# Layer statistics and normalisation of the later token pairs: VectorE's batch-norm instructions, or ScalarE passes with an accumulator

## The chip, the core and the metric

The kernel runs on one core of one Trainium2 chip. The time is device time in microseconds for one execution of the program. A core has TensorE (matrix products, PE in the profile; PEld is its loading of weights), VectorE (DVE), ScalarE (ACT), GpSimd (POOL) and SyncE (SP), each with its own queue of instructions, which it works off in order; semaphores make one engine wait for another. TensorE writes PSUM banks, which VectorE and ScalarE read and write.

## The reference, cut to what matters

```
def _layernorm(x):                       # over the 512 features of a token
    mu = jnp.mean(x, axis=-1, keepdims=True)
    var = jnp.mean(jnp.square(x - mu), axis=-1, keepdims=True)
    return (x - mu) / jnp.sqrt(var + EPS)
...
shift, scale, gate_msa = jnp.split(silu(t) @ ada_w + ada_b, 3, axis=1)
norm = where(m, _layernorm(x) * (1.0 + scale) + shift, 0.0)
ssm_out = where(m, ssm(norm) + flipped bwd(norm), 0.0)
x = x + gate_msa * ssm_out
shift_mlp, scale_mlp, gate_mlp = jnp.split(silu(t) @ ffada_w + ffada_b, 3, axis=1)
ff_norm = _layernorm(x) * (1.0 + scale_mlp) + shift_mlp
h = gelu(ff_norm @ ff_w1 + ff_b1)        # 512 -> 1024, tanh form
return x + gate_mlp * (h @ ff_w2 + ff_b2)  # 1024 -> 512
```

x is 32 batches of 128 tokens with 512 features, in float32. This case is about the second `_layernorm`, the one ahead of the feed-forward products.

## The kernel before, in words

The first half (the masked tokens through the two small networks) is done for the chosen tokens alone, and its rows are written to DRAM. The second half, the feed-forward block over all 4096 tokens, fills the time from about 83 us to the end. It goes in 4 pairs (`p`): a pair is two sides of 4 batches, so 2 x 4 tiles of 128 tokens x 512 features. Each of the two products of a pair is computed by seven half-sized block products P1 to P7 in place of eight, with sums of blocks formed by VectorE, GpSimd and ScalarE.

*First product* (`FirstProduct`): seven streams, in the order `STREAMS = (1, 2, 5, 6, 3, 7, 4)`. Each stream `j` has two PSUM banks, `e` and `a`. A *window* `w` interleaves the stream `STREAMS[w]` (new) with the one before (old): step n = 0 to 6 is new P5, new P1, old P3, old P7, new P2, new P6, old P4. After each step the work that belongs to it is issued: a copy of `e` by ScalarE (L1137), an addition by VectorE into `e` (L1167 behind P1, L1148 behind P6), into `h` (L1153 behind P7, L1158 behind P4), copies or gelus by ScalarE behind P2 and P3 (L1181, L1085), late sums by GpSimd (L1174, L1203, L1207). A bank may be written by the next product only when these have read it.

*Second product* (`SecondProduct`): `ORDER` lists its 14 steps, P1U P5U P1V P5V P2U and so on. P5V reads block sums `s1[1]`, which `first_block(1, 2, 4)` and `first_block(1, 0, 2)` (L1257, VectorE) form from gelus of the first product. The first steps of the second product are interleaved with P3, P7 and P4 of the last stream, stream 4.

*Where the next pair's tokens are normalised.* All orders are written out by hand: an engine runs its instructions in the order in which the program issues them. `put(w, n, f)` files work behind step n of window w. During pair p < 3 the tiles of pair p + 1 are gathered (`take_first_half`, GpSimd DMAs), then `Statistics.one(i)` takes mean and variance of a tile with VectorE's `bn_stats` and `bn_aggr` (L922, L923), and `root` adds EPS (L927, VectorE) and takes the power -0.5 for four tiles (L928, GpSimd). `blocks(side, i)` normalises a tile (L934, VectorE) and turns it in blocks of 32 x 32 (L1481, `nc.vector.transpose`). For side 0 the four calls of `blocks` stand between the last steps of stream 4, for p > 0 thus:

```
now.late_gelu("21")
blocks(0, 0); blocks(0, 1)
now.do(4, "P3"); second.seed(1); now.do(4, "P7")
second.first_block(1, 2, 4)
blocks(0, 2)
second.step(1, late=True); now.do(4, "P4")
blocks(0, 3)
second.load_gate(1); second.first_block(1, 0, 2)
second.seed_and_second_block(0)
```

For p = 0 `blocks(0, 0)` stands there alone ahead of P3, `blocks(0, 1)` behind P7, `blocks(0, 2)` behind P4 and `blocks(0, 3)` behind `first_block(1, 0, 2)`. Side 1 is normalised in the second product's steps 2 and 3. DMAs (`to_feature_rows`, L961, from SP's and ScalarE's queues) then bring the turned blocks to rows of features, ScalarE applies scale and shift (L944), and VectorE forms the block sums of the next first product (L991). The first pair's tokens are normalised apart from this, by other functions that the change leaves alone.

Of the kernel before, what the change touches and what calls it, by code (L numbers as in the profile page):

```python
# [9 lines left out]
F32 = mybir.dt.float32  # L10
# [3 lines left out]
AF = mybir.ActivationFunctionType  # L14
ALU = mybir.AluOpType
AX = mybir.AxisListType

EPS = 1e-6
# [4 lines left out]
def kernel(  # L23
# [49 lines left out]
    nc = tc.nc  # L73
    B, S, D = x.shape
    P = 128
    assert S == P
    G = 4
# [13 lines left out]
    stp = ctx.enter_context(tc.tile_pool(name="stp", bufs=4))  # L91
# [86 lines left out]
    def group_of_tiles(name):  # L178
        return xnp.tile([P, G, D], F32, tag="xn", name=f"xn_{name}")
# [35 lines left out]
    def project(i, h, w, name, between=None, bank=(ps_o, "o"), seeded=None):  # L215

        pool, tag = bank
        po = seeded or pool.tile([P, 512], F32, tag=tag, name=f"po_{name}_{i}")
        for f in range(HC):
            if between and f in between:  # L220
                between[f]()
            nc.tensor.matmul(  # L222
                po,
                h[f][:, ts(i, P)],
                w[:, f, :],
                start=(f == 0 and seeded is None),
                stop=(f == HC - 1),
                skip_group_check=seeded is not None,
            )
        return po  # L230
# [6 lines left out]
    def gated(po, bias, gate, name):  # L237

        t = tp.tile([P, D], F32, tag="t", name=f"t_{name}")
        nc.vector.tensor_tensor(t, po, bias, ALU.add)  # L240
        nc.vector.tensor_tensor(t, t, gate, ALU.mult)
        return t
# [144 lines left out]
    class Weights:  # L387


        def __init__(self, w, rows, cols, t):  # L390
            b11, b12 = w[:, :rows, :cols], w[:, :rows, cols:]
            b21, b22 = w[:, rows:, :cols], w[:, rows:, cols:]
            t2, t3, t4 = (t[:, j] for j in range(3))
            self.sums = [(t3, b22, b12), (b12, b12, b11), (t2, b22, b12), (t4, b21, t2)]
            self.of = {
                "P1": b11, "P2": b21, "P3": b22, "P4": t4, "P5": b12, "P6": t2, "P7": t3
            }
# [321 lines left out]
    def in_blocks(t):  # L719
        return t.rearrange("p g (h f) -> p (g h) f", f=2 * P)  # L720
# [59 lines left out]
    for f in range(KC):  # L780
        hidden_of_tile(f, 1)
        for done in (f - 1, f) if f % 2 else ():
            t = ssm.tile([P, NH], F32, tag="h", name=f"h_s0_{done}", bufs=HC)
# [28 lines left out]
    t = in_blocks(group_of_tiles("tw_3"))  # L812
# [27 lines left out]
    def in_turned_blocks(t):  # L840
        return t.rearrange("p i d -> p (i d)").rearrange("p (k i c) -> p k i c", i=G, c=P)

    def normalised(row, t):
        src = row[:, :D]
        if len(t.shape) == 3:
            src = src.rearrange("p (k c) -> p k c", k=KC)
        nc.vector.tensor_scalar(
            t, src, row[:, D : D + 1], row[:, D + 1 : D + 2], ALU.subtract, ALU.mult
        )
        return t  # L850
# [3 lines left out]
    def normalised_of_side_0(which):  # L854
        for i in which:
            t = normalised(raw[i // 2][:, i % 2], xn[:, :, i])
            nc.vector.transpose(t, t)
# [51 lines left out]
    class Statistics:  # L909


        def __init__(self, src, name):
            self.src, self.name = src, name
            self.mv = stp.tile([P, G, 2], F32, tag="mv4", name=f"mv_{name}", bufs=2)
            self.rstd = stp.tile([P, G], F32, tag="rstd4", name=f"rstd_{name}", bufs=2)

        def tile_at(self, i):
            return self.src[i // 2][:, i % 2]

        def one(self, i):  # L920
            st = stp.tile([P, 6], F32, tag="st", name=f"st_{self.name}_{i}")
            nc.vector.bn_stats(st, self.tile_at(i))  # L922
            nc.vector.bn_aggr(self.mv[:, i, :], st)  # L923

        def root(self):
            ve = stp.tile([P, G], F32, tag="ve4", name=f"ve_{self.name}", bufs=2)
            nc.vector.tensor_scalar(ve, self.mv[:, :, 1], EPS, None, ALU.add)  # L927
            nc.gpsimd.tensor_tensor(self.rstd, ve, half[:, :G], ALU.pow)  # L928

        def normalised(self, i, t):  # L930
            src = self.tile_at(i)
            if len(t.shape) == 3:
                src = src.rearrange("p (k c) -> p k c", k=KC)
            nc.vector.tensor_scalar(  # L934
                t, src, self.mv[:, i, 0:1], self.rstd[:, i : i + 1], ALU.subtract, ALU.mult
            )
            return t

# [15 lines left out]
    def turned(xn, xT, queues, which=range(4)):  # L954

        R = 32
        src = xn.rearrange("p k i (q c) -> p q k i c", c=R)
        dst = xT.rearrange("p k (i b c) -> p b k i c", b=P // R, c=R)
        for b in which:
            for q in range(P // R):  # L960
                queues[(b + q // 2) % len(queues)].dma_start(dst[ts(q, R), b], src[ts(b, R), q])  # L961
# [7 lines left out]
    def new_xT(p, side):  # L969
        return xtp.tile([P, KC, G * S], F32, tag=f"xT{side}", name=f"xT_{p}_{side}")  # L970
# [390 lines left out]
    def normalised_of_side_1():  # L1361
        t = sp.tile([P, G, D], F32, tag="s12", name="xn_0_1")
        for i in range(G):
            xn_b.append(normalised(raw[2 + i // 2][:, i % 2], t[:, i]))
# [42 lines left out]
    gp = straight.enter_context(tc.tile_pool(name="gp", bufs=1))  # L1407
# [26 lines left out]
    for p in range(NP):  # L1434
# [4 lines left out]
        def put(w, n, f, *args):  # L1439
            fills.setdefault(w, {}).setdefault(n, []).append(lambda: f(*args))  # L1440
# [26 lines left out]
        if more_pairs:  # L1467
            x_next = x_of[p + 1]
            stats = [Statistics(x_next[side], f"{p + 1}_{side}") for side in range(2)]
            xn, xT = {}, {}  # L1470

            def blocks(side, i):

                if i == 0:
                    xn[side] = in_turned_blocks(
                        group_of_tiles(f"{p + 1}_0")
                        if side == 0
                        else sp.tile([P, G, D], F32, tag="s12", name=f"xn_{p + 1}_1")
                    )
                t = stats[side].normalised(i, xn[side][:, :, i])  # L1480
                nc.vector.transpose(t, t)  # L1481

            def to_feature_rows(side, *queues):
                xT[side] = new_xT(p + 1, side)
                turned(xn[side], xT[side], queues)

            if p:
                put(1, 6, take_first_half, p + 1, x_next, range(G))
            put(2, 6, take_first_half, p + 1, x_next, range(G, G + 2 + (p == 0)))
            if p:  # L1490
                put(3, 4, take_first_half, p + 1, x_next, range(G + 2, G + 3))
            put(5, 4, take_first_half, p + 1, x_next, range(G + 3, 2 * G))
            for i, at in enumerate(((3, 1), (3, 3), (3, 4), (4, 1))):
                put(*at, stats[0].one, i)
            put(*((4, 1) if p else (5, 4)), stats[0].root)
            for i, at in enumerate(((4, 4), (5, 1), (5, 3), (6, 4))):
                put(*at, stats[1].one, i)
            put(6, 6, stats[1].root)
        for w in range(1 + (p == 0), 7):
            now.window(STREAMS[w], STREAMS[w - 1], fills.get(w, {}))  # L1500
# [88 lines left out]
    with tc.If(more > 0):  # L1589
# [11 lines left out]
        with tc.For_i(0, more, 1):  # L1601
# [12 lines left out]
            for half_no, (mod, was, wbs, bias, bcol, func) in enumerate(  # L1614
# [19 lines left out]
                shift, scale, gate_l = (mod_l[:, m] for m in range(3))  # L1634
# [5 lines left out]
                t = gated(project(0, h_l, wb, f"l{half_no}"), bias, gate_l, f"l{half_no}")  # L1640
# [59 lines left out]
```

## Time and profile before

| what | before |
|---|---|
| median of 3 runs | 453.1 us (452.22 to 453.49) |
| span of the profiled execution | 451.7 us, 6204 instructions |
| PE, PEld busy | 444.0 us (98%), 370.2 us (82%) |
| DVE busy | 334.5 us (74%), 573 instructions |
| ACT busy | 177.9 us (39%), 389 instructions |
| POOL busy | 158.4 us (35%), 154 instructions |
| granted TensorE clock | 1.000 |

The span runs from the first to the last instruction of the one execution that was profiled; the times are of other executions, from outside, and hold what lies around the span as well, here some 1.4 us between the two. Rows of the timeline give start, duration, engine, line of the kernel, operation, tile written `<-` tiles read, shapes and count; in brackets stands the idle time of the engine before it and what ended it. Rows of groups give count, busy us, mean ns of one, then idle time before them. A matmul's row begins some 0.17 us before the one ahead of it ends, since they are pipelined. Rows of consecutive instructions overlap on ScalarE and VectorE also, by some 0.07 to 0.1 us.

### The profile page before, as it was taken

The numbers are of one execution on the slowest core, as the hardware profiler recorded it, in microseconds if no ns is written. First come the engines' busy times: TensorE is split into PE (matmuls) and PEld (weight loads), VectorE is DVE, ScalarE is ACT, GpSimd is POOL, SyncE is SP. The second block draws the span as 40 slices with busy tenths as digits, with TensorE's granted clock in tenths as the row PEclk, the third lists the DMA queues.
The fourth block names the chain that finished last, engine by engine and source line by source line (L and its number), as shares of the span: only waits on it lengthen the run. The fifth ranks groups of instructions, "written<-read, shape, count | busy, mean of one in ns | idle before, by whom it ended". The sixth has DMA issues, their size and how long they took to land.

```text
span 451.7 us, 6204 instructions
## 1 busy us (share of the span) xinstructions
PE 444.0 (98%) x2147; PEld 370.2 (82%) x2147; DVE 334.5 (74%) x573; ACT 177.9 (39%) x389; POOL 158.4 (35%) x154
## 2 busy tenths in 40 slices
PE   8999999999999999999999999999999999999995
PEld 3884675688888888888888888888888888888884
DVE  5797788877799759977895689878956885434645
ACT  3123116353651551536526415464265244642000
POOL 4211470089770000897600007977000027560000
PEclk9999999999999999999999999999999999999999
DMA  6999449857327717741396177512971534122022
GB/s 250 372 399 408 177 65 308 284 187 229 129 97 168 108 49 268 235 138 36 105 177 93 46 267 230 141 38 86 189 99 47 176 128 129 35 93 95 0 94 96
DMA packets 85440, 70.84 MB, mean 157 GB/s; under 512 B 63396, under 2 KB 64508, under 8 KB 84382
## 3 DMA queue, kind: packets, MB, share of 16 engines
q1 hardware_dynamic: 64270, 57.76, 42.3%
q0 software_dynamic: 4160, 10.54, 6.9%
q10 hardware_dynamic: 16976, 2.11, 3.9%
q8 instruction: 18, 0.29, 0.3%
q14 instruction: 16, 0.13, 0.1%
HBM read 56.71 MB, written 13.70 MB: 156 GB/s over the span
## 4 chain that ended last, share of the span: by engine, by line
PE 84%; DMA 8%; DVE 3%; issue 2%; POOL 1%; SPq 0%; POOLq 0%
PE a_o L1310 24%; PE a_m L1123 21%; PE e_o L1310 18%; PE e_m L1123 16%; DMA fw<-in_L_cond_ff_w_dram 3%; PE po_s L222 3%; DMA w<-in_L_cond_bwd_w_dram 3%; DMA x_wide<-t_s 2%; DMA x<-x_wide,slot_i 1%; DVE t L403 1%; PE last L1310 1%; PE a_m_alone L1123 1%; POOL x L819 1%; PE ptr L950 0%; PE pl_s L255 0%
## 5 line engine op out<-in xcount | busy, mean ns | idle before, releaser
L1174 POOL TENSOR_TENSOR ha<-p_m,ha 128x512 f32<-128x512 f32 x20 | 25.8, 1292 | 176.0 <-ACT ha L1181 166.1
L1310 PE MATMUL e_o<-fw,ha 128*128 128x256 f32 x256 | 57.9, 379 | 0.0
L944 ACT ACTIVATE xT<-xT,modT 128x128 f32<-128x128 f32 x112 | 44.0, 480 | 28.1 <-DMA xT<-xn 28.1
L1310 PE MATMUL a_o<-t,hb 128*128 128x256 f32 x240 | 54.1, 379 | 0.0
L1310 PEld LDWEIGHTS e_o<-fw,ha 128*128 128x128 f32 x256 | 48.6, 190 | 6.6
L1310 PEld LDWEIGHTS a_o<-t,hb 128*128 128x128 f32 x240 | 45.6, 190 | 6.2
L1085 ACT ACTIVATE hb<-hb,biasT 128x256 f32<-128x256 f32 x64 | 29.0, 500 | 28.3 <-POOL hb L1207 16.1
L1137 ACT COPY p_m<-e_m 128x512 f32<-128x512 f32 x27 | 15.8, 586 | 51.6 <-PE e_m L1123 51.6
L890 POOL DMA_INDIRECT x<-x_rows,slot_i x24 | 27.2, 1135 | 6.2 <-issue 5.4
L1174 POOL TENSOR_TENSOR hb<-p_m,hb 128x512 f32<-128x512 f32 x20 | 29.2, 1460 | 0.3
L1310 PE MATMUL a_o<-fw,ha 128*128 128x256 f32 x128 | 28.9, 379 | 0.0
L1310 PE MATMUL a_o<-t,s 128*128 128x256 f32 x128 | 28.9, 379 | 0.0
L1310 PE MATMUL e_o<-fw,s 128*128 128x256 f32 x128 | 28.9, 379 | 0.0
L222 PE MATMUL po_s<-w,h_s 128*128 128x512 f32 x64 | 28.4, 594 | 0.0
L1181 ACT COPY ha<-e_m 128x512 f32<-128x512 f32 x32 | 18.5, 579 | 24.8 <-PE e_m L1123 24.4
L1310 PEld LDWEIGHTS a_o<-fw,ha 128*128 128x128 f32 x128 | 24.3, 190 | 3.3
L1310 PEld LDWEIGHTS a_o<-t,s 128*128 128x128 f32 x128 | 24.3, 190 | 3.3
L1310 PEld LDWEIGHTS e_o<-fw,s 128*128 128x128 f32 x128 | 24.3, 190 | 3.3
L1148 DVE TENSOR_TENSOR e_m<-a_m,ha 128x512 f32<-128x512 f32 x20 | 14.0, 698 | 17.0 <-POOL ha L1174 7.6
L1085 ACT ACTIVATE ha<-e_m,biasT 128x256 f32<-128x256 f32 x48 | 20.0, 468 | 14.4 <-PE e_m L1123 14.4
L1123 PE MATMUL a_m<-xT,tw 128*128 128x256 f32 x96 | 24.7, 380 | 0.0
L1123 PE MATMUL e_m<-s,fw 128*128 128x256 f32 x92 | 23.7, 380 | 0.0
(234 smaller groups left out, 894.1 us busy)
## 6 DMA issues: line engine op xcount, KB each, us to landing
x<-in_x_dram SPq DMA_DIRECT2D x16, 512.0 KB, 5.9
tw<-t_rows SPq DMA_DIRECT2D x16, 512.0 KB, 4.3
gate<-gate_rows POOLq DMA_DIRECT2D x8, 1024.0 KB, 5.1
out_dram<-x SPq DMA_DIRECT2D x15, 512.0 KB, 4.7
tw<-t_rows SPq DMA_DIRECT2D x16, 384.0 KB, 3.9
xT<-xn SPq DMA_DIRECT2D x80, 64.0 KB, 2.7
ada_f<-in_L_cond_ffada_w_dram SPq DMA_DIRECT2D x4, 768.0 KB, 14.8
ada_a<-in_L_cond_ada_w_dram SPq DMA_DIRECT2D x4, 512.0 KB, 3.6
```

Source lines behind the costliest of these rows:

```text
L222: nc.tensor.matmul(po, h[f][:, ts(i, P)], w[:, f, :], start=(f == 0 and seeded is None), stop=(f == HC - 1), skip_group_check=seeded is no ...
L403: engine.tensor_tensor(out, x, y, ALU.subtract)
L819: nc.gpsimd.indirect_dma_start(out=raw[i // 2][:, i % 2], out_offset=None, in_=x1_wide[:slots], in_offset=bass.IndirectOffsetOnAxis(ap=slo ...
L890: nc.gpsimd.indirect_dma_start(out=xs[i // G][i % G // 2][:, i % 2], out_offset=None, in_=x1_rows, in_offset=bass.IndirectOffsetOnAxis(ap= ...
L944: nc.scalar.activation(out, src, AF.Identity, bias=shift, scale=scale)
L1085: nc.scalar.activation(dst[:, n], src[:, n], AF.Gelu_apprx_tanh, bias=biasT[:, f : f + 1])
L1123: nc.tensor.matmul(bank[:, ts(n, QT)], self.w_block(j, product)[:, ts(n, P)], self.x_block(j, product), start=(product in ("P1", "P5") and ...
L1137: nc.scalar.copy(p5, e)
L1148: nc.vector.tensor_tensor(e, a, p5, add)
L1174: nc.gpsimd.tensor_tensor(self.place(RESULT[j], c), self.p5[j], other, ALU.add)
L1181: nc.scalar.copy(self.place(RESULT[j], c), src)
L1310: nc.tensor.matmul(part, src[:, k, ts(i, P)], w[product][:, k, :], start=(last and k == 0), stop=True, skip_group_check=True,)
```

## The change

For the tiles of pairs 2 to 4, ScalarE reads a tile once with Identity and an accumulator for the sum (`one`), VectorE turns the sum into minus the mean (one column), ScalarE reads the tile again with Square, that column as bias and an accumulator for the sum of squares (`two`). Both passes write their 512-wide result to a tile that nobody reads. `root` divides, adds EPS (VectorE), takes the power and forms `shift` = -mean x rstd (GpSimd). `normalised` is a ScalarE Identity with scale and bias columns; the 32 x 32 transpose behind it stays on VectorE. For p > 0 `root` of side 0 moves from (4, 1) to (4, 4).

```diff
         def __init__(self, src, name):
             self.src, self.name = src, name
-            self.mv = stp.tile([P, G, 2], F32, tag="mv4", name=f"mv_{name}", bufs=2)
+            self.sums = stp.tile([P, G], F32, tag="sums4", name=f"sums_{name}", bufs=2)
+            self.minus = stp.tile([P, G], F32, tag="minus4", name=f"minus_{name}", bufs=2)
+            self.var = stp.tile([P, G], F32, tag="var4", name=f"var_{name}", bufs=2)
             self.rstd = stp.tile([P, G], F32, tag="rstd4", name=f"rstd_{name}", bufs=2)
+            self.shift = stp.tile([P, G], F32, tag="shift4", name=f"shift_{name}", bufs=2)
...
+        def unread(self):
+            return gp.tile([P, D], F32, tag="unread", name=f"unread_{self.name}", bufs=1)
+
         def one(self, i):
-            st = stp.tile([P, 6], F32, tag="st", name=f"st_{self.name}_{i}")
-            nc.vector.bn_stats(st, self.tile_at(i))
-            nc.vector.bn_aggr(self.mv[:, i, :], st)
+            nc.scalar.activation(
+                self.unread(), self.tile_at(i), AF.Identity, accum_out=self.sums[:, i : i + 1]
+            )
+            nc.vector.tensor_scalar(
+                self.minus[:, i : i + 1], self.sums[:, i : i + 1], -1.0 / D, None, ALU.mult
+            )
+
+        def two(self, i):
+            nc.scalar.activation(
+                self.unread(),
+                self.tile_at(i),
+                AF.Square,
+                bias=self.minus[:, i : i + 1],
+                accum_out=self.var[:, i : i + 1],
+            )

         def root(self):
             ve = stp.tile([P, G], F32, tag="ve4", name=f"ve_{self.name}", bufs=2)
-            nc.vector.tensor_scalar(ve, self.mv[:, :, 1], EPS, None, ALU.add)
+            nc.vector.tensor_scalar(ve, self.var, 1.0 / D, EPS, ALU.mult, ALU.add)
             nc.gpsimd.tensor_tensor(self.rstd, ve, half[:, :G], ALU.pow)
+            nc.gpsimd.tensor_tensor(self.shift, self.rstd, self.minus, ALU.mult)

         def normalised(self, i, t):
...
-            nc.vector.tensor_scalar(
-                t, src, self.mv[:, i, 0:1], self.rstd[:, i : i + 1], ALU.subtract, ALU.mult
+            nc.scalar.activation(
+                t, src, AF.Identity, bias=self.shift[:, i : i + 1], scale=self.rstd[:, i : i + 1]
             )
             return t
...
             for i, at in enumerate(((3, 1), (3, 3), (3, 4), (4, 1))):
                 put(*at, stats[0].one, i)
-            put(*((4, 1) if p else (5, 4)), stats[0].root)
+            for i, at in enumerate(((4, 1), (4, 3), (4, 3), (4, 4))):
+                put(*at, stats[0].two, i)
+            put(*((4, 4) if p else (5, 4)), stats[0].root)
             for i, at in enumerate(((4, 4), (5, 1), (5, 3), (6, 4))):
                 put(*at, stats[1].one, i)
+            for i, at in enumerate(((5, 4), (5, 5), (6, 4), (6, 6))):
+                put(*at, stats[1].two, i)
             put(6, 6, stats[1].root)
```

## The prediction

> **What bounds the kernel now.** I read the page first, then busy time by stretches, the waits of TensorE's weight loads (PEld) behind the opening, and the timelines of the engines through one pair of sides. The rows of the page:
>
> ```profile
> span 451.7 us, 6204 instructions
> ...
> PE 444.0 (98%) x2147; PEld 370.2 (82%) x2147; DVE 334.5 (74%) x573; ACT 177.9 (39%) x389; POOL 158.4 (35%) x154
> ...
> PE 84%; DMA 8%; DVE 3%; issue 2%; POOL 1%; SPq 0%; POOLq 0%
> ```
>
> Busy time by stretches (columns: length, then PE, PEld, DVE, ACT, POOL, granted clock, DMA share, GB/s), and the waits of PEld from 80 us on (total, times, longest):
>
> ```profile
> 178.00:267.00 89.00, 89.00 (x413) 77.78 (x411) 71.19 (x109) 41.28 (x91) 36.07 (x30) 1.00 0.54 139
> ```
>
> ```profile
> PEld a_m L1123 <- DVE hb L1153: 1.1, 4, 0.4
> ```
>
> The reader is to see that TensorE is never out of work between pairs: 89.00 of 89.00 us, and about a microsecond of real waiting in all. So work taken from VectorE can pay at most that microsecond, while each new wait of TensorE is paid in full. The question is not whether ScalarE has room on average (41 of 89 us) but whether, in its fixed order, it delays what TensorE needs next.
>
> **The change part by part.** What VectorE loses, in groups (count, busy us, mean ns), with the row of the transposes that stay and that of a one-column scalar operation:
>
> ```profile
> L1481 DVE STREAM_TRANSPOSE xn<-xn 128x512 f32<-128x512 f32 x24 | 17.1, 712 | 0.8
> L922 DVE BATCH_NORM_STATS2 st<-x 128x6 f32<-128x512 f32 x24 | 16.4, 682 | 0.0
> L934 DVE TENSOR_SCALAR xn<-x,mv,rstd 128x512 f32<-128x512 f32 x24 | 14.7, 613 | 0.0
> L927 DVE TENSOR_SCALAR ve<-mv 128x4 f32<-128x4 f32 x6 | 6.0, 1006 | 0.1
> L923 DVE BATCH_NORM_AGGREGATE mv<-st 128x2 f32<-128x6 f32 x24 | 4.4, 182 | 0.8
> L162 DVE TENSOR_SCALAR ve_s<-mv_s 128x1 f32<-128x1 f32 x4 | 0.6, 154 | 0.1
> ```
>
> It loses 16.4 + 4.4 + 14.7 = 35.5 us and gets 24 one-column products, 24 x 0.154 = 3.7 us. ScalarE gets 72 passes. Their prices come from these rows:
>
> ```profile
> L944 ACT ACTIVATE xT<-xT,modT 128x128 f32<-128x128 f32 x112 | 44.0, 480 | 28.1 <-DMA xT<-xn 28.1
> L1181 ACT COPY ha<-e_m 128x512 f32<-128x512 f32 x32 | 18.5, 579 | 24.8 <-PE e_m L1123 24.4
> L1386 ACT ACT_TABLE_LOAD x1 | 1.3, 1283 | 0.0
> L570 ACT ACTIVATE s_sb<-t_sb 32x512 f32<-32x512 f32 x1 | 0.6, 630 | 0.2 <-DMA t_sb<-in_cond_dram 0.2
> L575 ACT COPY sT<-ptr_s 128x128 f32<-128x128 f32 x1 | 0.3, 265 | 1.6 <-PE ptr_s L574 1.6
> ```
>
> The two copies give (579 - 265)/384 = 0.82 ns per element. A normalisation is the 128-wide Identity of L944 (scale and bias from columns) widened to 512: 480 + 384 x 0.82 = 795 ns, followed by the next after about 0.71. A sum pass is L570's 0.63 us; a squared pass with a bias column lies between that and 0.80, I take 0.72. How the accumulator is written out, no row shows: between nothing and the 0.27 of a small copy, I take 0.1 of ScalarE's time and 0.2 until the sum can be read, near its small rows. Together 24 x (0.73 + 0.82 + 0.71) = 54 us on ScalarE, 18 per pair.
>
> *Statistics, windows 3 to 6.* ScalarE's waits there are holes of about a microsecond between copies that TensorE needs, and each takes one pass. Replayed by hand for the second iteration (p = 1), pass by pass at these prices: the copies behind P3 and P2 come 0.1 to 0.8 us later, for which the next reader has more than a microsecond. Two places are tight. First, today's only clear stall here goes. VectorE's `ve` sits before the addition behind P7 of stream 6, and TensorE waits for that:
>
> ```profile
> 199.48 1.10 DVE L927 TENSOR_SCALAR ve<-mv 128x4 f32<-128x4 f32 x1
> ...
> 203.00 0.70 DVE L1148 TENSOR_TENSOR e_m<-a_m,ha 128x512 f32<-128x512 f32 x1 [1.00 <-POOL ha L1203]
> ```
>
> ```profile
> 201.23 1.13 PE L1123 MATMUL a_m<-xn_sy,tw 128*128 128x256 f32 x4
> ...
> 203.93 1.03 PE L1123 MATMUL e_m<-s,fw 128*128 128x256 f32 x4
> ```
>
> `ve` began at 199.48 and took 1.10 us; products follow each other every 0.86, and the one at 201.23 is followed by the next at 202.20, so 0.2 us were lost. With `root` moved behind, that is won. Second, VectorE now has `ve` and the product for side 1's first tile ahead of L1148. Both wait for ScalarE, where the fourth squared pass and side 1's first sum pass stand behind the gelu of P2: about 202.4 and 203.2. L1148 then starts at 203.3 instead of 203.00 and ends at 204.0, past 203.93 less the 0.2 just won: 0.2 to 0.4 lost. I book these two as zero for p = 1 and 2. For p = 0, whose `root` is not at that place and which had no such stall, I book 0.2.
>
> *Normalisation, start of the second product.* Here is the price. Today VectorE normalises and transposes alone, in between products' additions, while ScalarE works beside it. Its transposes now wait for ScalarE, where each normalisation stands behind a gelu; and the gelu behind it waits for VectorE's addition, which stands behind the transpose. ScalarE before, p = 1 (and the one row of p = 0):
>
> ```profile
> 220.04 0.91 ACT L1085 ACTIVATE hb<-hb,biasT 128x256 f32<-128x256 f32 x2 [2.14 <-POOL hb L1207]
> 220.86 0.82 ACT L1085 ACTIVATE ha<-e_m,biasT 128x256 f32<-128x256 f32 x2
> 221.57 0.59 ACT L1249 COPY a_o<-fb 128x512 f32<-128x512 f32 x1
> ...
> 222.84 0.91 ACT L1085 ACTIVATE hb<-hb,biasT 128x256 f32<-128x256 f32 x2 [0.17 <-DVE hb L1153]
> 225.22 0.91 ACT L1085 ACTIVATE hb<-hb,biasT 128x256 f32<-128x256 f32 x2 [1.47 <-DVE hb L1158]
> ```
>
> ```profile
> 129.98 0.91 ACT L1085 ACTIVATE hb<-hb,biasT 128x256 f32<-128x256 f32 x2 [2.98 <-POOL hb L1207]
> ```
>
> VectorE before:
>
> ```profile
> 220.33 0.71 DVE L1481 STREAM_TRANSPOSE xn<-xn 128x512 f32<-128x512 f32 x1
> ...
> 222.16 0.65 DVE L1153 TENSOR_TENSOR hb<-a_m,hb 128x512 f32<-128x512 f32 x1
> ...
> 224.53 0.65 DVE L1158 TENSOR_TENSOR hb<-a_m,hb 128x512 f32<-128x512 f32 x1
> ...
> 226.30 0.65 DVE L1257 TENSOR_TENSOR s<-hb 128x512 f32<-128x512 f32 x1
> ```
>
> TensorE before, p = 1 and then p = 0: P4 of stream 4, which overwrites the bank L1153 reads, and P5V, whose first weights are what the last L1257 writes:
>
> ```profile
> 222.92 1.07 PE L1123 MATMUL a_m<-xT,tw 128*128 128x256 f32 x4
> ...
> 227.28 3.62 PE L1310 MATMUL e_o<-fw,s 128*128 128x256 f32 x16
> ```
>
> ```profile
> 132.01 1.03 PE L1123 MATMUL a_m<-xT,tw 128*128 128x256 f32 x4
> ...
> 136.32 3.62 PE L1310 MATMUL e_o<-fw,s 128*128 128x256 f32 x16
> ```
>
> Today L1257 ends at 226.95, 0.33 us ahead of 227.28. The new order for p = 1, counted from t, the start of the late gelu (220.04 above). It occupies ScalarE 0.82.
> 1. Normalise tile 0 from t+0.82, tile 1 from t+1.53, done at t+2.33 (ScalarE). Transpose 1 from t+2.38 to 3.05 (0.64 to 0.71 us each).
> 2. L1153 to t+3.70; so P4 starts at t+3.75. ScalarE meanwhile: gelu pair to 3.06, two seeds to 4.1, so L1153's gelu pair runs from 4.02, and tile 2's normalisation from 4.84 to 5.64.
> 3. Transpose 2 to 6.35; L1158 to 7.00; its gelu pair 7.05 to 7.95, tile 3's normalisation from 7.87 to 8.67; transpose 3 from 8.70 to 9.40; L1257 to 10.05. P5V at t+10.1.
>
> With t = 220.04 P5V starts at 230.14, 2.9 us late; TensorE idles about 0.9 ahead of P4 and 2.0 ahead of P5V. t itself moves: the late gelu waits for GpSimd's chain of late sums, which starts with the copy behind P3 of stream 7, now some 0.7 later behind squared passes and seeds. The row of its last link:
>
> ```profile
> 218.75 1.26 POOL L1207 TENSOR_TENSOR hb<-hb 128x512 f32<-128x512 f32 x1
> ```
>
> Between 0 and 0.7, I take 0.35, since part of the chain waits for other things: 3.2 us each for p = 1 and 2. In p = 0 one tile is normalised at each place and the last L1257 stands behind three of them, each behind a gelu pair: tile 0 done t+1.62, transpose 2.35, L1153 3.00, gelu pair 3.3 to 4.2, tile 1 done 4.9, transpose 5.65, two additions 6.95, gelu pair to 7.9, tile 2 done 8.62, transpose 9.35, L1257 10.0, P5V at t+10.05. With t = 129.98 + 0.35 that is 140.4 against 136.32: 4.1 us.
>
> *Side 1 and after.* Its four normalisations are in steps 2 and 3, behind the four DMA issues of side 0 on ScalarE's queue; the fourth transpose comes about 0.4 us later against TensorE than now. The next product's P5 has 258.37 - 254.48 = 3.9 us in hand there, between the sum that it reads (VectorE) and its start (TensorE):
>
> ```profile
> 253.25 1.23 DVE L991 TENSOR_TENSOR s<-xT 128x1024 f32<-128x1024 f32 x1 [3.63 <-ACT xT L944]
> ```
>
> ```profile
> 258.37 1.03 PE L1123 MATMUL e_m<-s,fw 128*128 128x256 f32 x4
> ```
>
> So zero; if that cover is gone, each microsecond costs one. SP's queue issues the same DMAs. The throw-away output tile is written by ScalarE alone and waits for nobody. GpSimd gets six 128x4 products (`shift`), each between 0.1 and the 1.04 of the root:
>
> ```profile
> 200.66 1.04 POOL L928 TENSOR_TENSOR rstd<-ve,half 128x4 f32<-128x4 f32 x1
> ```
>
> Nearer the low end, as a power costs more than a product; zero beside the t above, to 0.9 per pair in the range.
>
> *The sum.* 4.1 + 3.2 + 3.2 + 0.2 = 10.7 us on a span of 451.7: 462.4. The median of the runs, 453.1, is 1.4 above that span (launch and spread); carried over, 463.8, which I round to 463.5.
>
> **The rivals.**
>
> *One-column products held up by GpSimd.* The row to look at is `ve`: 0.14 us in p = 0, where GpSimd had nothing in hand, but 1.10 above, where GpSimd was in an addition until 200.55:
>
> ```profile
> 116.44 0.14 DVE L927 TENSOR_SCALAR ve<-mv 128x4 f32<-128x4 f32 x1
> ```
>
> ```profile
> 199.28 1.27 POOL L1174 TENSOR_TENSOR hb<-p_m,hb 128x512 f32<-128x512 f32 x1
> ```
>
> If the 24 one-column products behave so, each costs up to 1.2 us. Three of them have no cover: side 1's first, ahead of L1148, puts P3 of stream 3 back by 1 us in each pair, and one at (6, 4) some 0.5. That is 3 to 4.5 us more: 467. Against it: no one-column product of this trace stood beside GpSimd's work, and the 0.154 row is without it. The Trainium skill (SBUF — State Buffer, "Who interferes with whom") says that VectorE's two-port modes and GpSimd lock each other out for a whole instruction, whoever is second waiting. `ve`'s 0.14 against 1.10 agrees; whether one column enters such a mode, no run here shows. Chance 0.15.
>
> *Tables.* Three table loads stand in the whole trace and Identity and Copy run between gelus without one; Square does not occur. If it needs another set, each squared pass or pair of them brings two loads of 1.283: some 18 x 2.57 = 46 us on ScalarE, of which, with holes of a microsecond, most of the half in windows 4 to 6 reaches TensorE: 485. The Trainium skill (ScalarE: Activation LUTs, "Table sets: the hidden batching unit") has cheap functions in every set; Square is not among the examples there, so this stays a rival. Chance 0.03.
>
> *No cost: the chain keeps its cover.* What decides is t: if GpSimd's chain gets shorter because VectorE no longer disputes with it, and the late gelu starts 2.9 us earlier (at 217.1 rather than 220.04), P5V is not late, the lost 0.2 us of p = 1 and 2 are won and the time is 452.7. For it speaks that L1207 at 218.75 is the end of a chain of GpSimd's additions, some of them beside VectorE's work; against it that this chain would have to lose more than two whole additions of 1.26 us, and that it starts later. Chance 0.06, of it 0.02 for more than 0.3% faster.
>
> **How the numbers follow.** The forecast has 0.76, the product rival 0.15, tables 0.03, cover kept 0.06. 0.3% is 1.4 us, about what a measurement of this kernel can tell from no change. The low end: t unmoved and normalisations as short as the 0.58 copies take 0.85 off each chain, so 3.0 + 2.0 + 2.0 = 7.0, or 460; the accumulator free, 459. The high end: the product rival, 467, with the late GpSimd products, 468.5. Faster 0.02, same 0.04, slower 0.94.
>
> **What would show it.** VectorE busy near 302 and ScalarE near 230 us. A wait of TensorE ahead of P4 of stream 4 near 1 us and ahead of P5V near 2, in three iterations and not in the fourth; VectorE's transposes waiting for ScalarE's normalisation; the 0.2 us stall behind `ve` gone. One-column products of a microsecond would show the first rival, ACT_TABLE_LOADs beyond three the second. It is wrong if P5V keeps its time, or if TensorE waits mostly in windows 3 to 6, where I booked next to nothing.

## The result and the profile after

| | before | changed |
|---|---|---|
| median of 4 runs each | 452.7 us (452.22 to 453.49) | 467.13 us (466.04 to 467.68) |
| ratio | 1 | 1.0309, 95% interval 1.0289 to 1.033 |
| span of the profiled execution | 451.7 us | 464.2 us |
| PE busy | 444.0 us | 446.6 us |
| DVE busy | 334.5 us | 306.3 us |
| ACT busy | 177.9 us | 226.5 us |

The change makes the kernel 3.1% slower: 14.4 us by the medians, 12.5 by the two profiled executions. VectorE has 28 us less to do and ScalarE 49 us more; neither is what the time goes by. The waits of TensorE itself from 80 us on (total, times, longest), of which the profile before has none:

```profile
PE e_o L1329 <- DVE s L1276: 5.8, 3, 2.3
PE a_m L1142 <- DVE hb L1172: 4.0, 3, 1.4
PE e_m L1142 <- DVE e_m L1167: 1.3, 3, 0.4
```

Three waits in each of three pairs: P5V for the last block sum (L1276, which was L1257), P4 of stream 4 for the addition ahead of it (L1172, was L1153), P3 of stream 3 for L1167 (was L1148). Lines behind the changed class are 19 higher than before. TensorE in the second iteration, with the idle time in front of each:

```profile
208.75 1.10 PE L1142 MATMUL e_m<-s,fw 128*128 128x256 f32 x4 [0.44 <-DVE e_m L1167]
...
229.38 1.13 PE L1142 MATMUL a_m<-xT,tw 128*128 128x256 f32 x4 [1.39 <-DVE hb L1172]
230.35 3.62 PE L1329 MATMUL a_o<-fw,ha 128*128 128x256 f32 x16
...
235.70 3.69 PE L1329 MATMUL e_o<-fw,s 128*128 128x256 f32 x16 [1.74 <-DVE s L1276]
```

Who waits for whom there is read off ScalarE and VectorE side by side. ScalarE, from the late gelu on:

```profile
225.69 0.91 ACT L1104 ACTIVATE hb<-hb,biasT 128x256 f32<-128x256 f32 x2 [1.42 <-POOL hb L1226]
226.50 1.50 ACT L953 ACTIVATE xn<-x,shift,rstd 128x512 f32<-128x512 f32 x2
...
229.66 0.91 ACT L1104 ACTIVATE hb<-hb,biasT 128x256 f32<-128x256 f32 x2
230.47 0.81 ACT L953 ACTIVATE xn<-x,shift,rstd 128x512 f32<-128x512 f32 x1
232.63 0.91 ACT L1104 ACTIVATE hb<-hb,biasT 128x256 f32<-128x256 f32 x2 [1.36 <-DVE hb L1177]
233.44 0.80 ACT L953 ACTIVATE xn<-x,shift,rstd 128x512 f32<-128x512 f32 x1
```

VectorE in the same time:

```profile
227.33 1.42 DVE L1500 STREAM_TRANSPOSE xn<-xn 128x512 f32<-128x512 f32 x2 [1.65 <-ACT xn L953]
228.67 0.65 DVE L1172 TENSOR_TENSOR hb<-a_m,hb 128x512 f32<-128x512 f32 x1
...
231.30 0.71 DVE L1500 STREAM_TRANSPOSE xn<-xn 128x512 f32<-128x512 f32 x1 [1.38 <-ACT xn L953]
231.94 0.65 DVE L1177 TENSOR_TENSOR hb<-a_m,hb 128x512 f32<-128x512 f32 x1
234.27 0.71 DVE L1500 STREAM_TRANSPOSE xn<-xn 128x512 f32<-128x512 f32 x1 [1.68 <-ACT xn L953]
234.90 0.65 DVE L1276 TENSOR_TENSOR s<-hb 128x512 f32<-128x512 f32 x1
```

The reader is to see two engines that take turns, three times each, from the late gelu to the block sum: VectorE is idle for 1.4 to 1.7 us ahead of each of its turns, ScalarE, which has copies to do in between, for 1.4 us ahead of its last. P5V starts when the last turn (L1276, ending at 235.55) is done.

From the starts of the four iterations on TensorE, the first pair costs 5.04 us more than before, the second 4.02, the third 4.03; with an opening 0.57 shorter that is the 12.5 us between the spans.

### The profile page after: what moved, and what is told of

It is laid out like the page before. It is cut to its first block, busy times and chain, and to the rows that moved or that the text cites. A ratio compares the mean times of both kernels' runs of the same rounds, so it can differ in the third digit from the quotient of the medians.

```text
span 464.2 us, 6305 instructions
## 1 busy us (share of the span) xinstructions
PE 446.6 (96%) x2147; PEld 369.9 (80%) x2147; DVE 306.3 (66%) x525; ACT 226.5 (49%) x509; POOL 158.3 (34%) x160
## 4 chain that ended last, share of the span: by engine, by line
PE 77%; ACT 11%; POOL 5%; issue 3%; DVE 3%; ACTq 0%; DVEq 0%
PE a_o L1329 19%; PE e_o L1329 16%; PE a_m L1142 13%; PE e_m L1142 11%; PE po_s L222 6%; PE ph_s L205 5%; ACT unread L935 2%; ACT hb L1104 2%; POOL hb L1226 2%; ACT xn L953 2%; PE ph_s L681 2%; ACT ha L1104 1%; ACT unread L927 1%; POOL hb L1193 1%; ACT ha L1200 1%
## 5 line engine op out<-in xcount | busy, mean ns | idle before, releaser
L1500 DVE STREAM_TRANSPOSE xn<-xn 128x512 f32<-128x512 f32 x24 | 17.0, 711 | 21.3 <-ACT xn L953 21.3
```

## The experiments

Theory A is the prediction's: the price is the alternation of the two engines ahead of P4 and P5V, with a small wait at P3. Rival B: ScalarE has too much to do, wherever the passes stand.

**Statistics alone.** The normalisation goes back to VectorE, and `shift` is not formed:

```diff
-            nc.scalar.activation(
-                t, src, AF.Identity, bias=self.shift[:, i : i + 1], scale=self.rstd[:, i : i + 1]
-            )
+            nc.vector.tensor_scalar(
+                t, src, self.minus[:, i : i + 1], self.rstd[:, i : i + 1], ALU.add, ALU.mult
+            )
```

> Statistics by ScalarE as in the change, normalisation back on VectorE. Theory A (the price is the alternation of ScalarE's normalisations with VectorE's transposes and additions at the start of the second product, 2.9 to 4.4 us a pair, with 0.4 to 0.7 us a pair at P3 of stream 3): P3's wait stays, 0.68 us three times; the start of the second product loses only what `ve`, now later, pushes back, 0.7 to 1.7 us a pair. Sum 3 to 6 us over before: 456 to 459 us. Rival B (the price goes with the time that ScalarE is taken, 48 us of passes, wherever they stand): the 48 statistics passes with their reads are 41 of 60 us, so about 10 of the 14 us: 462 to 463 us.

457.3 us against 453.17 of before, ratio 1.0089 (1.0073 to 1.0104). TensorE's waits from 80 us on (lines here are 17 higher than before the change: L1170 was L1153, L1165 was L1148):

```profile
PE a_m L1140 <- DVE hb L1170: 1.4, 2, 0.7
PE e_m L1140 <- DVE e_m L1165: 1.3, 3, 0.4
```

P5V does not wait; P3 waits as in the changed kernel, and P4 in two pairs, because VectorE comes later to its addition L1165 and to all that stands behind it, `ve` among it. Counted from the start of the second product, L1165 starts at 2.55 us (218.24 - 215.69) in the second iteration, where it was 1.48 (215.77 - 214.29) before; ahead of it VectorE stands waiting for ScalarE's sum of side 1's last tile:

```profile
218.13 0.15 DVE L929 TENSOR_SCALAR minus<-sums 128x1 f32<-128x1 f32 x1 [3.47 <-ACT unread L926]
```

Two thirds of ScalarE's new passes cost 4.1 of the 14.4 us, not 10: against B.

**Normalisation alone.** Statistics by VectorE as before, the shift column by two GpSimd products:

```diff
             nc.gpsimd.tensor_tensor(self.rstd, ve, half[:, :G], ALU.pow)
+            nc.gpsimd.tensor_scalar(self.shift, self.mv[:, :, 0], -1.0, None, ALU.mult)
+            nc.gpsimd.tensor_tensor(self.shift, self.shift, self.rstd, ALU.mult)
...
-            nc.vector.tensor_scalar(
-                t, src, self.mv[:, i, 0:1], self.rstd[:, i : i + 1], ALU.subtract, ALU.mult
-            )
+            nc.scalar.activation(
+                t, src, AF.Identity, bias=self.shift[:, i : i + 1], scale=self.rstd[:, i : i + 1]
+            )
```

> Statistics by VectorE as before, normalisation by ScalarE (the shift column formed by two small GpSimd products more). Theory A: the late gelu starts where it did before, P5V comes 10.1 us behind it, so 2.9 + 2.9 + 3.7 = 9.5 us over before, 0.3 less or more: 462 us; P3 of stream 3 does not wait, the waits ahead of P4 and P5V are 1 to 2.3 us. Rival B: 19 of 60 us of ScalarE's passes, so about 4.5 us: 457 us.

464.48 us, ratio 1.0241 (1.0225 to 1.0258): 11.3 us over before, with a third of the passes. B is out, but the forecast of 462 was 2.5 us too low, and P4 waited 0.6 to 0.9 us, not 1 or more. The chain has the length that was worked out: ScalarE's late gelu and TensorE's P5V of the second iteration are 10.01 us apart (forecast 10.1), and the gelu starts 5.75 us behind the start of the second product, as before (lines here are 3 higher than before the change).

```profile
225.78 0.91 ACT L1088 ACTIVATE hb<-hb,biasT 128x256 f32<-128x256 f32 x2 [2.13 <-POOL hb L1210]
```

```profile
235.79 3.69 PE L1313 MATMUL e_o<-fw,s 128*128 128x256 f32 x16 [1.73 <-DVE s L1260]
```

Most of the excess over 9.5 us in the profiled execution has its place in the first pair. There P5V took 5.38 us instead of 3.69 behind its wait, and the granted clock (the column with 1.00 in the first row) was 0.61 and 0.90 in these stretches:

```profile
139.89 5.38 PE L1313 MATMUL e_o<-fw,s 128*128 128x256 f32 x16 [2.33 <-DVE s L1260]
```

```profile
137.00:139.80 2.80, 0.56 (x3) 0.16 (x1) 1.34 (x3) 2.77 (x6) 0.00 (x0) 1.00 0.58 237
139.80:143.30 3.50, 3.41 (x10) 2.80 (x11) 2.81 (x3) 0.41 (x1) 0.00 (x0) 0.61 0.32 43
143.30:146.70 3.40, 3.40 (x16) 2.93 (x15) 1.78 (x3) 2.60 (x5) 0.00 (x0) 0.90 1.03 148
```

9.5 and this 1.7 are 11.2 us; the span is 11.8 longer than the one before, and the other 0.6 us stays open. Two other executions, at mean granted clocks of 0.998 and 0.997, which executions of the kernel before show as well, were 10.5 and 11.0 us over before; the lower clock does not explain what these have above 9.5.

**The wait at P3.** Side 1's first sum pass two steps later, in the changed kernel:

```diff
-            for i, at in enumerate(((4, 4), (5, 1), (5, 3), (6, 4))):
+            for i, at in enumerate(((4, 6), (5, 1), (5, 3), (6, 4))):
                 put(*at, stats[1].one, i)
```

> The changed kernel with side 1's first sum pass and its product on VectorE two steps later, at (4, 6) in place of (4, 4), behind the addition that P3 of stream 3 waits for. Theory A: that product, not the gelu or GpSimd's sums, holds the addition; the three waits of 0.44 us (0.68 with what the pipeline loses) go or shrink to 0.2, P4 and P5V keep theirs: 1 to 2 us under the changed kernel. Rival (the addition waits for GpSimd's late sum, as it did before): unchanged within 0.5 us.

464.94 us, ratio 1.0271 (1.0252 to 1.0289), 2.2 us under the changed kernel's median (and 1.1 to 2.1 by the executions at a clock of 1.000 alone). The waits for L1167 are gone, the others unchanged to the tenth:

```profile
PE e_o L1329 <- DVE s L1276: 5.8, 3, 2.3
PE a_m L1142 <- DVE hb L1172: 4.0, 3, 1.4
```

So it was VectorE's in-order wait for ScalarE's sum, not a GpSimd sum. In the changed kernel this is the place (VectorE):

```profile
207.80 0.15 DVE L930 TENSOR_SCALAR minus<-sums 128x1 f32<-128x1 f32 x1 [0.30 <-ACT unread L927]
207.91 0.70 DVE L1167 TENSOR_TENSOR e_m<-a_m,ha 128x512 f32<-128x512 f32 x1
```

**One link less.** The changed kernel in which VectorE normalises one of side 0's four tiles in each of the three pairs, the one whose transpose stands last:

```diff
+            if self.by_vector == i:
+                nc.vector.tensor_scalar(
+                    t, src, self.minus[:, i : i + 1], self.rstd[:, i : i + 1], ALU.add, ALU.mult
+                )
+                return t
...
+            stats[0].by_vector = 3 if p else 2
+            stats[1].by_vector = None
```

> The changed kernel, but the one tile of side 0 whose transpose stands last ahead of the final block sum (tile 3, in the first pair's iteration tile 2) is normalised by VectorE. Theory A, link by link: that tile no longer waits for the gelu pair ahead of it; VectorE normalises and turns it beside the gelu, so P5V comes 1.2 us earlier in each of three pairs: 3.6 us under the changed kernel, the wait ahead of P5V 0.6 to 1.2 us, the one ahead of P4 as it is. Rival B: one tile in eight of the normalisations, 0.8 us of 20 a pair, so under 0.7 us in all.

462.88 us, ratio 1.0208 (1.0195 to 1.0222): 4.2 us under the changed kernel's median, and 3.6, as expected, under the middle of its two executions at a clock of 1.000. P4 waits as it did, P5V 2.0 us in all instead of 5.8, so 1.27 less per pair where 1.2 was expected (lines here are 24 higher than before the change: L1177 was L1153, L1281 was L1257, L1172 was L1148):

```profile
PE a_m L1147 <- DVE hb L1177: 4.0, 3, 1.4
PE e_o L1334 <- DVE s L1281: 2.0, 3, 1.1
PE e_m L1147 <- DVE e_m L1172: 1.3, 3, 0.4
```

Three normalisations of 0.8 us, 2.4 us of ScalarE's time in all, were worth 3.8 us of waits, where rival B allowed 0.7: position, not load.

**All passes on ScalarE, in another order.** Normalisations (`normal`, ScalarE) apart from their transposes (`turn_blocks`, VectorE), which keep all their places; the other calls of `blocks` for side 0 become `turn_blocks` likewise:

```diff
-            def blocks(side, i):
+            def normal(side, i):
...
-                t = stats[side].normalised(i, xn[side][:, :, i])
+                stats[side].normalised(i, xn[side][:, :, i])
+
+            def turn_blocks(side, i):
+                t = xn[side][:, :, i]
                 nc.vector.transpose(t, t)
...
+        if more_pairs:
+            for i in range(2):
+                normal(0, i)
         now.late_gelu("21")
         if more_pairs:
             for i in range(1 + (p > 0)):
-                blocks(0, i)
+                turn_blocks(0, i)
         now.do(4, "P3")
         second.seed(1)
+        if more_pairs:
+            for i in range(2, G):
+                normal(0, i)
         now.do(4, "P7")
...
```

> The changed kernel with ScalarE's normalisations of side 0 issued apart from the transposes: tiles 0 and 1 ahead of the late gelu, where ScalarE sat idle 1.4 to 2.3 us, tiles 2 and 3 behind the seeds; VectorE's order is kept. Theory A: all 60 us of passes are still on ScalarE, but no transpose waits behind a gelu that waits for VectorE, so nearly all of the 3.6 to 4.4 us at P4 and P5V comes back, 0 to 0.5 a pair stays, and the three waits at P3 of stream 3 stay (0.44 us idle each): 1 to 3.5 us over before, 454 to 457 us. Rival B (ScalarE's load): no change beyond 1 us.

455.82 us, ratio 1.0066 (1.0052 to 1.0081): 11.3 of the 14.4 us are back with every pass still on ScalarE. Waits left:

```profile
PE e_m L1142 <- DVE e_m L1167: 1.3, 3, 0.4
PE e_o L1329 <- DVE s L1276: 0.4, 1, 0.4
```

With the later sum pass as well:

> The earlier normalisations and the later first sum pass together. Theory A: the effects add up; a further 1.5 to 2.2 us less than with the earlier normalisations alone, so 452.5 to 455 us: level with before, and not faster by more than the 0.5 us that its two stalls behind `ve` cost. Rival B: as the changed kernel.

454.25 us (12 runs), ratio 1.0030 (1.0017 to 1.0042). The two effects add up as far as can be told; one wait of 0.4 us ahead of the first pair's P5V and short waits of the weight loads are left, and it stays 1.1 us behind before. Lighter by 29 us (305.6 us busy), VectorE returns nothing.

**The clock.** Theory C was formed from the 0.61 above; two of four executions of the changed kernel were at a mean granted clock of 0.995 and 0.996, with spans of 465.9 and 465.7 us, the others at 1.000, with 464.2 and 465.1.

```diff
         for step in range(2, len(ORDER)):
+            if step == 3 and more_pairs:
+                busy = ps_t.tile([P, 512], F32, tag="tr", name=f"busy_{p}")
+                for _ in range(8):
+                    nc.tensor.matmul(busy[:, :P], ident, ident, start=True, stop=True)
             second.step(step)
```

> The changed kernel with eight 128x128 products on TensorE, whose result nobody reads, ahead of P5V in the three pairs, some 0.9 us of work within a gap of 1.7 to 2.5 us. Theory C: in some executions of the changed kernel and of the one with normalisation alone the granted clock falls behind the 2.33 us gap of the first pair and costs 1.2 to 1.7 us; with the gap cut to about 1.4 us this never happens: all executions at a clock of 0.998 or more, 465.5 to 467 us, the median 0.3 to 1 us under the changed kernel's. Rival D (the lower clock has nothing to do with the gap): about half the executions still at 0.994 to 0.996 and the median as the changed kernel's.

465.97 us (465.53 to 466.21), ratio 1.0287 (1.0274 to 1.0301); all five executions at 0.998 or more. The eight products took 1.95 us and not 0.9, so they filled more of the gap than was meant: P4's waits are the same as without them, P5V's is 0.56 us in the first pair and gone in the others, and P5V starts no later. That agrees with C: 1.2 us of the changed kernel's median, a little more than was expected.

Two executions of four and none of five are few, but all the runs here say the same. Mean granted clocks of 0.996 or less occur only in the three kernels whose profile has the gap of 2.33 us: in 2 of 4 executions of the changed kernel, 2 of 4 with normalisation alone, 2 of 5 with the later sum pass, and these took 0.6 to 1.8 us longer than the others of their kernel. In 67 executions of the other kernels, 23 of the kernel before among them, the lowest was 0.997. Only the profile of normalisation alone shows the drop in its place; that it stands at the same place in the changed kernel is probable and not shown.

**The stall of the kernel before.** `root` of side 0 at (5, 4) in all pairs, nothing else:

```diff
-            put(*((4, 1) if p else (5, 4)), stats[0].root)
+            put(5, 4, stats[0].root)
```

> The kernel before, with side 0's `root` at (5, 4) in every pair as it is in the first: the 0.24 us stall of TensorE behind `ve` goes in two pairs, 0.5 us under before (452.7 us), about what can be told from no change; the rival, GpSimd's chain moved by its power, 0 to 0.5 us slower.

452.14 us (12 runs) against 453.12 of before, ratio 0.9984 (0.9973 to 0.9995). This is the one version that is faster than both, by 0.05 to 0.27%, by taking away a wait of TensorE and not work from VectorE. In its profile the two iterations whose `root` was moved are 0.25 and 0.26 us shorter, which is the 0.5 that was expected; the rest of the 1.0 us between the medians is within the interval.

## Why the prediction was right, point by point

- *What bounds it.* TensorE's waits account for the difference: 11.1 us of idle time, and what the pipeline loses each time it starts again; 28 us less on VectorE gave back nothing, as the 89.00 of 89.00 said. The cover-kept rival and with it every gain is out.
- *Prices.* The passes took what was worked out from the narrower rows: 0.62 for a sum (0.63), 0.72 for squares (0.72), 0.80 for a normalisation (0.795); the accumulator is an instruction of its own of 0.19 (taken as 0.1 of ScalarE's time and 0.2 until the sum can be read). VectorE came to 306.3 us and ScalarE to 226.5, where 302 and 230 were forecast. A group row of ScalarE, and `shift` on GpSimd, where 0.1 to 1.04 was left open (minimum, median, maximum in ns):

```profile
L935 ACT ACTIVATION_READ_ACCUMULATOR unread<-x,minus 128x1 f32 x24 | 4.5, 188 | 0.0
```

```profile
L947 POOL TENSOR_TENSOR shift<-rstd,minus x6: 198/199/268, 121.5 to 321.9; 128x4 f32<-128x4 f32 x6
```

- *The chain.* P5V started 10.01 us behind the late gelu in the second iteration and 140.72 - 130.82 = 9.90 in the first; forecast 10.1 and 10.05. Experiments two and four confirm single links.
- *First term mis-sized: when the late gelu starts.* It was put 0.35 us later than before, between 0 and 0.7; measured from the start of the second product it is 225.69 - 219.19 = 6.50 against 5.75, and 0.75 later in the first pair too: just past the upper bound. GpSimd's late sums pass on the delay of the copy that starts them, 0.79 us at their start (218.78 - 219.19 against 213.09 - 214.29), almost whole; the part that "waits for other things" did not exist. 0.4 us a pair.
- *Second: P3 of stream 3.* The two effects there were booked as zero, 0.2 in the first pair. The wait is 0.44 us idle and 0.24 more that the pipeline loses in starting again, 0.68 in all (starts of TensorE's rows), against 0.24 won. The addition ended some 0.15 later than in the replay by hand, and the loss of restarting was left out. 0.45 us a pair. The gain was real: experiment eight shows it by itself.
- *The sum* was 10.7 us on the span and 13.1 came, 12.5 with the opening. The medians are 14.4 apart, since the changed kernel's profiled execution, 466.04 us for a span of 464.2, is the fastest of its four, and two of the four had the lower clock, which the prediction left out. The 1.4 us that it carried over from span to median was too little as well: an execution here takes 1.7 to 1.9 us longer than its span.
- *The range.* That 467.1 lies in it is in part luck. The forecast with t at its upper bound is about 1 us longer, near 465; the upper end came from the product rival, whose 467 is nearly the measured time, and from late GpSimd products, and neither occurred: these products took some 0.15 and 0.2 us each.
- *Rivals.* One-column products do not wait for GpSimd: all 24 took 149 to 156 ns, the one at 203.01 in the middle of a GpSimd addition (202.50 to 203.79). `ve`, with four columns, took 0.16 us in the first pair and 1.23 beside an addition, with which it ended (225.68 and 225.66). The rule cited from the Trainium skill agrees with that, and the runs answer what was open: one column is not held up. Square brought no table load; there are three, as before.

```profile
L930 DVE TENSOR_SCALAR minus<-sums x24: 149/153/156, 101.9 to 316.6; 128x1 f32<-128x1 f32 x24
```

## What to carry to other kernels

Before work is moved to an emptier engine, write the two queues side by side at the place where it lands: if the moved step stands between two steps of the other engine and itself behind a step that waits for that engine, the engines take turns, and each turn is paid, however idle both are. Splitting the moved step from its consumer and issuing it earlier, in a hole of the same queue, brought back 11.3 of 14.4 us here with not one instruction less on ScalarE. When the bound engine is full, look for its own short waits: one line moved gave 0.2 to 1.2 us here, 28 us less work on a neighbour nothing.

## What the runs showed of the hardware that was not expected

In the execution profiled with the normalisation alone, TensorE's granted clock fell to 0.61 in the 3.5 us behind an idle time of 2.33 us and cost 1.7 us (an idle time of 0.88 us stood 7 us ahead of it), while the same gap, with the clock at 1.00, stands in the profiled execution of the changed kernel:

```profile
140.70:144.00 3.30, 3.27 (x15) 2.94 (x16) 2.74 (x3) 0.34 (x1) 0.00 (x0) 1.00 0.27 45
```

So a gap of 2.33 us is enough, in some executions; in the ten executions of the two kernels whose longest wait from 80 us on is 1.4 us (one link less, and the gap filled), the clock stayed at 0.998 or more. The Trainium skill (TensorE: Matmul & The Clock Gate, "Part 1: The HAM clock gate (the "warmup" mystery)") gives about 3.4 us of idle time, in a window that runs freely; a free-running window agrees with the gap deciding in one execution and not in another, the length does not agree with 2.33, and here the measurement decides.
